# Attention inside a two-layer network: results of another head between a step's scores and sums, LN(x) tiles made in pairs and transposed a step later

## The chip, the cores and the metric

The kernel runs on one core of one Trainium2 chip. A core has a matrix engine (TensorE, in the profile PE, with its weight loads as PEld), three engines for everything else (VectorE, DVE; ScalarE, ACT; GpSimd, POOL) and SyncE (SP), which only issues DMAs. The engines run beside each other; each takes its own instructions in order and waits on semaphores for the others. The metric is the device time of one execution in microseconds (us); a lower time is better.

## The reference

Two layers on x of 4 x 32 x 32 tokens with 384 channels, all in float32. The part that the change touches is the first half of the first layer:

```python
qkv = _ln_c(x).reshape(B, N, C) @ qkv_w.T           # N = 1024 tokens, 12 heads of 32
attn = softmax(einsum('bhnd,bhmd->bhnm', q, k) * scale, axis=-1)
# 48 prototypes: every query chooses one; the mean query of each one marks 96 of the keys
final = row[..., :, None] * col[..., None, :]        # col: how many prototypes marked a key
attn = attn * final
attn = attn / (attn.sum(axis=2, keepdims=True) + 1e-08)   # over the queries
x = x + einsum('bhnm,bhmd->bhnd', attn, v)... @ proj_w.T
```

Then follow a mixture of four experts (two of them for a token), and a second layer with an outlook attention and a feed-forward part whose weights are Kronecker products. Attention is normalized twice: a softmax over the keys, then a division by the sum over the queries. So each score matrix is passed over twice, with two kinds of sums.

## The kernel before

`attention` walks through 4 images x 12 heads = 48 heads. A head is 4 steps (`PAIRS`), so there are 192 steps (`STEPS`), and the loop runs 9 more to finish. A step handles two blocks of 128 keys against all 1024 queries of a head. All instructions of TensorE, VectorE, ScalarE and SyncE are issued in the order in which the Python code writes them.

The parts of a step, with the names that the profile shows:

- **scores** (L597, tile `ps_s`): four matmuls, each on 32 rows of the array, into two PSUM tiles of 1024 columns. The pool `at_ps_s` has two such tiles, that is, one step's.
- **exps** (L607, tile `e`): two ScalarE instructions turn them into exponentials, in two tiles of the pool `at_e`.
- **total** (sums, L615 with tile `ps_z`): four matmuls, each on 32 columns of the array, add the exponentials up over the keys, in the one tile of `at_ps_z`.
- **gather** and **spread**: after a head's last sums, the sums go out to DRAM by two SyncE DMAs, come back in another layout, and their reciprocals are spread over all partitions (`rz`) by two more.
- **share** (L653 and L660): six steps later (`SHARE = 6`) VectorE multiplies the two tiles `e` in place with `rz` and with the column weights, sums them over the queries, and scales the values by the reciprocals, into `wv`.
- **out** (results, L615 with tile `ps_o`): seven steps later (`OUT = 7`) four matmuls with `wv` and the tiles `e` build the head's result in the one tile of `at_ps_o`. These are the last readers of the two tiles `e`.
- **keep** (L673, L680, L682): after a head's last results ScalarE copies `ps_o`, and four DMAs (two on SyncE, two adding ones on GpSimd) put the rows over those of the queries.

The pool of the exponentials has `EBUFS = 14` buffers. A tile's buffer is given to a new tile when all instructions that use the old one have been issued, and the new tile's first writer waits for the last of them on the chip.

Between the exponentials and the sums of a step, other work is put in. Some has fixed places: values (L690 to L695), projections of the image before (`project`), the loads and counts of the search for the 96 keys (`topk`: ScalarE's Sign at L351 once a step, its `load` at L306 and L310, `count` at L400). The rest comes from two generators, `groups` (prototypes: L517, L546, L561) and `prepare` (LN(x), then q and k). Each yields a cost in us and a condition before the next unit. In each step, units are taken while the account `spent` is below `goal`, and `goal` rises by `PACE = 2.6` a step but never to more than `MOST = 2.6` above `spent`, so a budget that is not used is lost:

```python
goal = min(goal + (RAMP if step < 12 else PACE), spent + MOST)
...
while spent < goal and prepared():
    pass
```

`prepare(b)` handles an image in two halves of four tiles of 128 tokens. For each half VectorE takes mean and variance, ScalarE the square root (L463), and then, tile by tile, ScalarE writes the normalized tile `xn` (L471, two buffers), TensorE transposes it (`turn`, L445, three blocks) into a PSUM tile, and ScalarE copies that into `xnT` (L446). After that come the q and k matmuls (L266), each followed by a copy (L501). The PSUM tiles of all this work come from `psum()`, which has two buffers. The transposes of a tile are issued behind the next tile's `xn`. `after(n)` is a condition that holds n steps after the unit became the next one.

Of the kernel before, what the change touches and what calls it, by code (L numbers as in the profile page):

```python
# [10 lines left out]
FP = mybir.dt.float32  # L11
AF = mybir.ActivationFunctionType
# [4 lines left out]
P = 128  # L17
B, IMG, C = 4, 32, 384
# [120 lines left out]
def attention(net, outer, router, x, x1, unsafe, qkv_wT, gpT, proj_wT, proj_w, gate_w, gate_b):  # L139
# [14 lines left out]
    tc, nc = net.tc, net.nc  # L154
    NHEAD = B * NH
    PAIRS = NB // 2
    STEPS = PAIRS * NHEAD
    SHARE, OUT = 6, 7
# [5 lines left out]
    with ExitStack() as ctx:  # L164
# [4 lines left out]
        work = ctx.enter_context(tc.tile_pool(name="at_work", bufs=2))  # L169
# [10 lines left out]
        def fetch(b, half, tag="xt"):  # L180
            xt = xts[b, half] = early.tile([P, 4, C], FP, name="xt", tag=tag)
            r = b * NTOK + 512 * half
            nc.sync.dma_start(out=xt, in_=x[r : r + 512, :].rearrange("(t p) c -> p t c", p=P))
# [58 lines left out]
        def gating():  # L242

            by = early.tile([P, KC, C], FP, name="proj", tag="xt")
            nc.scalar.dma_start(out=by, in_=proj_w.rearrange("(k p) i -> p k i", p=P))
            ps = psum()
            for k in range(KC):
                nc.tensor.matmul(
                    ps[:, :NE], lhsT=router.ones, rhs=gates[:, k, :], start=k == 0, stop=k == KC - 1
                )  # L250
            for c in range(KC):
                o = (c + 1) * NE
                for k in range(KC):
                    nc.tensor.matmul(
                        ps[:, o : o + NE], lhsT=by[:, k, c * P : (c + 1) * P], rhs=gates[:, k, :],
                        start=k == 0, stop=k == KC - 1,
                    )
            nc.scalar.copy(sums, ps[:, :NE])
            nc.scalar.copy(
                wproj[:, :, C:], ps[:, NE : (KC + 1) * NE].rearrange("p (c e) -> p c e", e=NE)  # L260
            )
# [18 lines left out]
        def after(steps):  # L280
            due = now[0] + steps
            return lambda: now[0] >= due

        spent = 0.0
        reached, heads, projected, valued = set(), [], set(), set()
# [141 lines left out]
        def prepare(b):  # L427

            im = images[b]
            yield 0, lambda: b == 0 or b - 1 in valued
            xnT = im["xnT"] = early.tile([P, KC, NTOK], FP, name="xnT", tag="xnT")
            for name in ("col", "inv"):
                im[name] = tiny.tile([P, NB, NH], FP, name=name, tag=name, bufs=2)
            nc.gpsimd.memset(im["col"], float(NG))
            im["mean"] = few.tile([P, NB], FP, name="mean", tag="mean", bufs=3)
            im["std"] = few.tile([P, NB], FP, name="std", tag="std", bufs=3)
            im["x"] = few.tile([P, NB, NE], FP, name="gate_x", tag="gate_x", bufs=3)  # L440

            def turn(xn, o):
                ps = psum()
                for c in range(KC):
                    nc.tensor.transpose(ps[:, c * P : (c + 1) * P], xn[:, c * P : (c + 1) * P], net.ident)  # L445
                nc.scalar.copy(xnT[:, :, o : o + P], ps[:, :C].rearrange("p (c t) -> p c t", c=KC))  # L446

            behind = None
            for half in range(2):
                if half and b:  # L450
                    yield 0, after(2)
                xt = xts.pop((b, half))
                mv = tiny.tile([P, 4, 2], FP, name="ln_mv", tag="ln_mv", bufs=2)
                rs = tiny.tile([P, 4], FP, name="ln_rs", tag="ln_rs", bufs=2)
                off = tiny.tile([P, 4], FP, name="ln_off", tag="ln_off", bufs=2)
                for t in range(4):
                    st = tiny.tile([P, 6], FP, name="ln_st", tag="ln_st", bufs=2)
                    nc.vector.bn_stats(st, xt[:, t, :])
                    nc.vector.bn_aggr(mv[:, t, :], st)
                    if t % 2:  # L460
                        yield 0.3, None
                std = im["std"][:, 4 * half : 4 * half + 4]
                nc.scalar.activation(std, mv[:, :, 1], AF.Sqrt, bias=net.eps["c"])  # L463
                yield 0.3, after(1) if b else None
                nc.vector.tensor_copy(im["mean"][:, 4 * half : 4 * half + 4], mv[:, :, 0])
                nc.vector.reciprocal(rs, std)
                nc.vector.scalar_tensor_tensor(off, mv[:, :, 0], -1.0, rs, ALU.mult, ALU.mult)
                for t in range(4):
                    yield 0.9, None
                    xn = work.tile([P, C], FP, name="xn", tag="xn")  # L470
                    nc.scalar.activation(  # L471
                        xn, xt[:, t, :], AF.Identity, bias=off[:, t : t + 1], scale=rs[:, t : t + 1]
                    )
                    if behind is not None:
                        turn(*behind)
                    behind = xn, (4 * half + t) * P
                if half == 0 and b:
                    fetch(b, 1)
                elif half and b + 1 < B:
                    if b == 0:  # L480
                        gating()
                    fetch(b + 1, 0)
            yield 0.9, None
            turn(*behind)
            for c in range(KC):
                yield 0, lambda: (
                    (b == 0 or len(heads) > NH * (b - 1) + 4 * c + 3)
                    and (b < 2 or len([p for p in projected if p[0] == b - 2]) == NB)
                )
                q = lasting.tile([P, NTOK], FP, name="q", tag="q", bufs=6)  # L490
                k = big.tile([P, NTOK], FP, name="k", tag="k", bufs=3)
                im["q"].append(q)
                im["k"].append(k)
                for out, base in ((q, 0), (k, C)):
                    for half in range(2):
                        yield 2.6, None
                        cols = slice(half * 512, half * 512 + 512)
                        ps = psum()
                        o = base + c * P
                        linear(ps, lambda k: wqkv[:, k, o : o + P], lambda k: xnT[:, k, cols])  # L500
                        nc.scalar.copy(out[:, cols], ps)  # L501
                reached.add((b, c, "qk"))
# [301 lines left out]
        step = -100  # L804
# [17 lines left out]
        goal = spent  # L822
        for step in range(STEPS + OUT + 2):
            n, u = divmod(step, PAIRS)
            if 0 <= step - OUT < STEPS:
                heads[(step - OUT) // PAIRS].out((step - OUT) % PAIRS)
                if (step - OUT) % PAIRS == PAIRS - 1:
                    heads[(step - OUT) // PAIRS].keep()
            if n < NHEAD:
                heads[n].scores(u)  # L830
            if u == 0 and 0 < n <= NHEAD:
                heads[n - 1].gather()
            if n < NHEAD:
                heads[n].exps()
            b, i = divmod(step, PAIRS * NH)
            goal = min(goal + (RAMP if step < 12 else PACE), spent + MOST)
            if u == 1 and 0 < n <= NHEAD:
                heads[n - 1].spread()
            begin(step)
            if step < 12:  # L840
                search()
                search()
            widen(step)
            o, t = i - OUT - 2, (i - OUT - 2) // 2
            if b and 0 <= o < 2 * NB and o % 2 == 0:
                project(b - 1, t)
            if b and 0 <= o + 1 < 2 * NB and o % 2:
                residue(b - 1, t + 1)
            if b and o > 2 * NB:
                next(routing[b - 1], None)  # L850
            if b < B:
                for t in {3: [0], 4: [1, 2], 5: [3], 6: [4], 7: [5, 6], 8: [7]}.get(i, []):
                    value(b, t)
            while spent < goal and prepared():
                pass
            if n < NHEAD:
                heads[n].total(u)
            if zeros and step >= 4:
                zeros.pop(0)()
            if 0 <= step - SHARE < STEPS:  # L860
                heads[(step - SHARE) // PAIRS].share((step - SHARE) % PAIRS)
            search()
            end()
            search()
            if u == 1 and n + 1 < NHEAD:
                heads.append(Head(n + 1))
# [1330 lines left out]
```

## Time and profile before

| what | value |
|---|---|
| median of 3 runs | 3002.94 us (3001.56 to 3003.22) |
| the profiled execution | 3008.57 us |
| its span, first to last instruction | 3006.7 us, granted TensorE clock 0.971 |
| TensorE (PE) busy | 2793.6 us, 93% |
| VectorE (DVE) busy | 1344.4 us, 45% |
| ScalarE (ACT) busy | 1222.3 us, 41% |
| GpSimd (POOL) busy | 396.4 us, 13% |
| first scores, last scores of the attention loop | 81.4 us, 1252.8 us |

Busy time is the union of an engine's instructions. In the timeline a line gives the start, the length, the engine, the line of the code, the operation with the tile that it writes and those that it reads, its tile of the array (for TensorE, rows x columns) and shape, and how many instructions are merged into it; in brackets stands the idle time before it and what ended it. One float32 matmul of the code shows as two records. In the table of waits a line gives who waited for what, the total, the number of times and the longest. In the table by stretch there are, for each engine, the busy time and the number of instructions, then the granted clock of TensorE, the share of the DMA engines and GB/s.

### The profile page before, as it was taken

The page shows a single profiled execution, that of the slowest core. Times are in us where ns is not written, and L with a number is a line of the kernel's source. Part 1 is how long each engine was busy: PE and PEld are TensorE (multiplying, and loading weights), DVE is VectorE, ACT ScalarE, POOL GpSimd, SP SyncE. Part 2 cuts the span into 40 slices and gives each one's busy share as a digit, 9 for nine tenths or more (in the row PEclk, how much of TensorE's full clock was granted, in tenths as well). Part 3 has the DMA queues.
Part 4 walks back from the last instruction along what each step waited for, and adds up shares of the span by engine and source line. Part 5 has one row for each costly group of instructions (what it writes and reads, how often), then busy time and mean ns, then how long its engine had stood idle before and what let it go on. Part 6 is the DMA issues. An engine that isn't in the chain of part 4 may idle for free.

```text
span 3006.7 us, 36661 instructions
## 1 busy us (share of the span) xinstructions
PE 2793.6 (93%) x13236; PEld 1509.9 (50%) x13236; DVE 1344.4 (45%) x3704; ACT 1222.3 (41%) x2026; POOL 396.4 (13%) x496
## 2 busy tenths in 40 slices
PE   6879998999899986689999999999999978999998
PEld 4323333333333331156777777777777744444443
DVE  1466677766776676633010001111111147767652
ACT  3777777776767765321112112111121122222125
POOL 1000000200030004014111112212211012000000
PEclk9989999999999998899999999999999989999999
DMA  5133334322322233254445545555555455544432
GB/s 100 52 81 98 92 92 122 78 54 68 93 56 54 77 90 118 49 200 155 169 177 189 186 174 204 213 211 196 201 215 210 142 170 190 163 165 139 157 112 86
DMA packets 218111, 405.91 MB, mean 135 GB/s; under 512 B 83504, under 2 KB 179296, under 8 KB 204864
## 3 DMA queue, kind: packets, MB, share of 16 engines
q1 hardware_dynamic: 188496, 194.43, 21.7%
q0 software_dynamic: 26432, 206.01, 20.1%
q10 hardware_dynamic: 2992, 3.03, 0.3%
q8 instruction: 107, 1.75, 0.2%
q14 instruction: 84, 0.69, 0.1%
HBM read 305.35 MB, written 49.99 MB: 118 GB/s over the span
## 4 chain that ended last, share of the span: by engine, by line
PE 78%; ACT 7%; DVE 6%; DMA 5%; issue 4%; POOL 0%; SPq 0%; DVEq 0%; POOLq 0%; ACTq 0%
PE ps_h L1568 18%; PE ps_y L1583 17%; PE ps_t L266 7%; PE ps_z L615 7%; PE ps_s L597 6%; PE ps_o L615 5%; PE ps_a L1693 4%; ACT e L607 4%; PE ps_y L1795 3%; DVE e L653 2%; PE ps_wo L1811 2%; DMA yt<-yg,index 2%; PE ps_v L1737 1%; PE ps_h L1964 1%; PE ps_t L400 1%
## 5 line engine op out<-in xcount | busy, mean ns | idle before, releaser
L1572 ACT ACTIVATE h<-ps_h,up 128x256 f32<-128x256 f32 x420 | 199.0, 474 | 929.2 <-PE ps_h L1568 929.2
L1568 PE MATMUL ps_h<-xbT,up 128*128 128x256 f32 x2520 | 556.8, 382 | 0.8 <-DVE xbT L1527 0.7
L1583 PE MATMUL ps_y<-down,h 128*128 128x384 f32 x1680 | 556.8, 489 | 0.0
L1568 PEld LDWEIGHTS ps_h<-xbT,up 128*128 128x128 f32 x2520 | 482.4, 192 | 76.9 <-DVE xbT L1527 1.1
L653 DVE CUSTOM_DVE_ANT_0 e<-e,rz,inv 128x1024 f32<-128x1024 f32 x384 | 474.3, 1272 | 65.1 <-DMA rz<-r_row 64.8
L607 ACT ACTIVATE e<-ps_s,shift 128x1024 f32<-128x1024 f32 x384 | 406.7, 1110 | 192.2 <-PE ps_s L597 191.9
L1583 PEld LDWEIGHTS ps_y<-down,h 128*128 128x128 f32 x1680 | 318.5, 191 | 208.2 <-issue 3.3
L1588 DVE TENSOR_TENSOR y<-ps_y,down 128x384 f32<-128x384 f32 x70 | 39.0, 558 | 755.6 <-PE ps_y L1583 755.6
L615 PE MATMUL ps_z<-e,rt_ones 128*32 128x512 f32 x1536 | 295.1, 631 | 62.8 <-ACT e L607 62.8
L615 PE MATMUL ps_o<-e,wv 128*32 128x512 f32 x1536 | 273.9, 634 | 27.2 <-DVE wv L660 15.6
L597 PE MATMUL ps_s<-q,k 32*128 32x512 f32 x1536 | 222.9, 650 | 0.0
L680 POOL DMA_DIRECT2D q<-po x96 | 75.7, 874 | 1058.2 <-DMA q<-po 622.2
L351 ACT ACTIVATE below<-tk_left,tk_bound 128x1024 bf16<-128x1024 f32 (+1 forms) x160 | 183.8, 1149 | 12.1 <-DVE tk_bound L357 7.6
L1693 PE MATMUL ps_a<-wa,xnT 128*128 128x486 f32 x384 | 172.2, 595 | 10.7 <-DVE attn L1703 10.0
L615 PEld LDWEIGHTS ps_z<-e,rt_ones 128*32 128x32 f32 x1536 | 45.6, 109 | 228.4 <-ACT e L607 190.0
L597 PEld LDWEIGHTS ps_s<-q,k 32*128 32x128 f32 x1536 | 61.5, 187 | 169.5 <-issue 135.1
L615 PEld LDWEIGHTS ps_o<-e,wv 128*32 128x32 f32 x1536 | 66.4, 114 | 150.5 <-issue 108.7
L266 PE MATMUL ps_t<-xnT,wqkv 128*128 128x512 f32 x288 | 138.1, 621 | 2.8 <-ACT tk_left L310 1.8
L1693 PEld LDWEIGHTS ps_a<-wa,xnT 128*128 128x128 f32 x384 | 72.4, 195 | 96.7 <-issue 89.6
L1795 PE MATMUL ps_y<-band,v 128*32 128x194 f32 (+2 forms) x960 | 108.4, 516 | 4.1 <-DMA band<-room 3.9
L1538 DVE SCALAR_TENSOR_TENSOR x<-yt,weight,x 128x384 f32<-128x384 f32 x38 | 23.5, 619 | 191.9 <-DMA x<-x 191.3
L1507 POOL DMA_INDIRECT xb<-x,ids x70 | 66.9, 955 | 251.4 <-PE ps_t L1526 218.4
(331 smaller groups left out, 2860.6 us busy)
## 6 DMA issues: line engine op xcount, KB each, us to landing
band<-room SPq DMA_DIRECT2D x32, 1560.0 KB
rz<-r_row SPq DMA_DIRECT2D x48, 512.0 KB
yg<-y SPq DMA_DIRECT2D x70, 192.0 KB
q<-q SPq DMA_DIRECT2D x192, 64.0 KB
k<-k SPq DMA_DIRECT2D x192, 64.0 KB
room<-none SPq DMA_DIRECT2D x64, 192.0 KB
x<-x SPq DMA_DIRECT2D x38, 192.0 KB
o<-in_x_dram SPq DMA_DIRECT2D x33, 192.0 KB
```

Source lines behind the costliest of these rows:

```text
L266: nc.tensor.matmul(ps, lhsT=lhsT(k), rhs=rhs(k), start=k == 0, stop=k == KC - 1)
L351: nc.scalar.activation(junk[:n], left[:n], AF.Sign, bias=bound[:n], accum_out=over[:n])
L597: nc.tensor.matmul(ps[:, half * 512 : half * 512 + 512], lhsT=self.k4[r, u * P : (u + 1) * P], rhs=self.q4[r, :], start=True, stop=True,)
L607: nc.scalar.activation(e, ps, AF.Exp, bias=shift, scale=QK_SCALE)
L615: nc.tensor.matmul(ps[r : r + 32, :], lhsT=lhsT(odd), rhs=self.es[2 * u + odd][:, half * 512 : half * 512 + 512], start=u == 0, stop=u == ...
L653: nc.vector.tensor_tensor_reduce(self.es[m], self.es[m], self.rz, 1.0, self.im["inv"][:, m, self.h : self.h + 1], ALU.mult, ALU.add, self. ...
L680: nc.gpsimd.dma_start(out=there, in_=po[r : r + 32, :], accum_op=ALU.add)
L1568: nc.tensor.matmul(ps, lhsT=up[:, o : o + P], rhs=xbT[:, k, :], start=k == 0, stop=k == KC - 1,)
L1572: nc.scalar.activation(h, ps, AF.Gelu, bias=up[:, KC * HID + f : KC * HID + f + 1])
L1583: nc.tensor.matmul(ps, lhsT=hs[f][:, t * P : (t + 1) * P], rhs=down[:, f * C : (f + 1) * C], start=f == 0, stop=f == NF - 1,)
L1693: nc.tensor.matmul(pa[:, hh, :HW_], lhsT=xnT[:, k, :], rhs=wa[:, k, hh * HW_ : (hh + 1) * HW_], start=k == 0, stop=k == KC - 1,)
L1795: nc.tensor.matmul(ys[c][32 * n : 32 * n + 32, lo - 512 * half : hi - 512 * half], lhsT=vs[b, t][:, h * HD : (h + 1) * HD], rhs=bands[b, t ...
```

## The change

In the step loop, the results of seven steps before (`out`, and `keep` when a head ends) are issued after the scores, the gather and the exponentials of the step, where they were issued before the scores. In `prepare`, a unit makes two tiles `xn` where it made one, and it begins with the transposes of the two tiles that the unit before made. From the second image on, such a unit comes at the earliest one step after the unit before. The costs follow: five units of 1.8 in an image, where there were nine of 0.9.

```diff
-            behind = None
+            behind = []
...
-                for t in range(4):
-                    yield 0.9, None
-                    xn = work.tile([P, C], FP, name="xn", tag="xn")
-                    nc.scalar.activation(
-                        xn, xt[:, t, :], AF.Identity, bias=off[:, t : t + 1], scale=rs[:, t : t + 1]
-                    )
-                    if behind is not None:
-                        turn(*behind)
-                    behind = xn, (4 * half + t) * P
+                for two in range(2):
+
+                    yield 1.8, after(1) if b else None
+                    while behind:
+                        turn(*behind.pop(0))
+                    for t in (2 * two, 2 * two + 1):
+                        xn = work.tile([P, C], FP, name="xn", tag="xn")
+                        nc.scalar.activation(
+                            xn, xt[:, t, :], AF.Identity, bias=off[:, t : t + 1], scale=rs[:, t : t + 1]
+                        )
+                        behind.append((xn, (4 * half + t) * P))
...
-            yield 0.9, None
-            turn(*behind)
+            yield 1.8, after(1) if b else None
+            while behind:
+                turn(*behind.pop(0))
...
             n, u = divmod(step, PAIRS)
-            if 0 <= step - OUT < STEPS:
-                heads[(step - OUT) // PAIRS].out((step - OUT) % PAIRS)
-                if (step - OUT) % PAIRS == PAIRS - 1:
-                    heads[(step - OUT) // PAIRS].keep()
             if n < NHEAD:
                 heads[n].scores(u)
             if u == 0 and 0 < n <= NHEAD:
                 heads[n - 1].gather()
             if n < NHEAD:
                 heads[n].exps()
+            if 0 <= step - OUT < STEPS:
+                heads[(step - OUT) // PAIRS].out((step - OUT) % PAIRS)
+                if (step - OUT) % PAIRS == PAIRS - 1:
+                    heads[(step - OUT) // PAIRS].keep()
```

## The prediction

> **What bounds the kernel now.** I read the page's totals first, then TensorE's waits in the attention stage, then the timeline of single steps.
>
> ```profile
> PE 2793.6 (93%) x13236; PEld 1509.9 (50%) x13236; DVE 1344.4 (45%) x3704; ACT 1222.3 (41%) x2026; POOL 396.4 (13%) x496
> ```
>
> TensorE is the busy engine, but this is an average over stages. The change touches only the attention loop, whose 192 steps run from 81 to 1257 us. There, from 123 us on (the first results) to 1255 us, the waits of TensorE are:
>
> ```profile
> PE ps_z L615 <- ACT e L607: 57.9, 63, 3.0
> PE ps_t L445 <- ACT xn L471: 25.4, 10, 4.3
> ...
> PE ps_o L615 <- DVE topped L390: 5.6, 1, 5.6
> ```
>
> The columns are total us, times and longest. Sums wait for exponentials, and the transposes of LN(x) wait for their tile: the two things that the change moves. How a step runs is seen in two kinds of steps. The first has plenty of other matmuls:
>
> ```profile
> 657.59 1.06 PE L615 MATMUL ps_z<-e,rt_ones 128*32 128x512 f32 x8
> 658.48 1.04 PE L615 MATMUL ps_o<-e,wv 128*32 128x512 f32 x8
> 659.45 1.14 PE L597 MATMUL ps_s<-q,k 32*128 32x512 f32 x8
> 660.52 0.70 PE L266 MATMUL ps_t<-xnT,wqkv 128*128 128x512 f32 x1
> ```
>
> From start to start, sums take 0.89, results 0.97, scores 1.07, then other work follows without a gap. Ninety-eight of the 184 steps 7 to 190 are longer than the floor shown next. The second kind has little other work:
>
> ```profile
> 302.71 1.14 PE L597 MATMUL ps_s<-q,k 32*128 32x512 f32 x8
> 303.78 0.92 PE L546 MATMUL ps_t<-gpbd,q 128*128 128x192 f32 x4
> 305.05 1.63 PE L615 MATMUL ps_z<-e,rt_ones 128*32 128x512 f32 x6 [0.35 <-ACT e L607]
> 306.07 0.62 PE L615 MATMUL ps_o<-e,wv 128*32 128x512 f32 x2
> ...
> 307.90 0.71 PE L597 MATMUL ps_s<-q,k 32*128 32x512 f32 x4
> ```
> ```profile
> 303.89 2.12 ACT L607 ACTIVATE e<-ps_s,shift 128x1024 f32<-128x1024 f32 x2 [1.95 <-PE ps_s L597]
> ```
>
> Scores at 302.71, exponentials from 303.89 to 306.01, the second half of the sums and the results behind it, the next scores at 307.90: 5.19 us. Eighty-six steps have this length to 0.05 us whatever else they hold; it is the ring scores, exponentials, sums, results, scores.
>
> **The new order in a step.** Its aim is to let results (four calls, eight records) fill the wait for the exponentials. One number stands against that. A step makes two e tiles, results run OUT = 7 steps behind their scores, and EBUFS = 14. In the old order the results of step s-7 have been issued when step s takes its two tiles. In the new order `exps` asks for them while `out(s-7)`, the last reader of the two oldest, is still ahead: all 14 are live. So ScalarE's exponentials wait for the results, and behind them in ScalarE's queue everything else of the step: the copy of ps_o, which now follows them, copies out of PSUM, the search's Sign. TensorE's sums wait for all of it. The ring keeps its members in another order: scores, results, exponentials, sums. Its length from the rows: scores to results 1.07; results end 1.04 after they start and the exponentials follow a matmul's end by 0.04 (302.71 + 1.14 to 303.89), so they start at 2.15 and end at 4.27; the second half of the sums starts 0.06 later (306.01 to 306.07) and holds TensorE for two of its passes and a change to the scores' shape, 0.44 + 0.53 = 0.97: 5.30 us, 0.11 more than 5.19.
>
> In the 98 longer steps the change of the array's tile shape counts. In a step of the old order that has other work the shape changes three times (128*128 to 128*32, to 32*128, and back; sums and results share one shape), in the new order four times. The first steps, which have no results yet, show sums between two changes:
>
> ```profile
> 112.74 1.07 PE L615 MATMUL ps_z<-e,rt_ones 128*32 128x512 f32 x8
> 113.74 1.14 PE L597 MATMUL ps_s<-q,k 32*128 32x512 f32 x8
> ```
>
> That is 1.00 instead of 0.89. Results between two changes are not in this trace; by the same row they take 1.00 instead of 0.97. Sums and results then take 2.00 instead of 1.86: 0.14 a step. Results into 128*128 could cost as little as 0.97 or as much as the scores' 1.07, so the bounds are 0.10 and 0.24; 1.00 is the same operation, so I take it. Sum: 86 x 0.11 + 98 x 0.14 = 9.5 + 13.7 = 23 us.
>
> Something comes back where results were late for another reason. TensorE waited 15.0 us in 11 waits for VectorE before results; the scores now run meanwhile, at most 1.07 each, 7.7 us together; half of it, 4, since VectorE's lateness also reaches the next step. Where ScalarE itself is late (before 29 of the 192 pairs of exponentials it was not idle for scores), results hide; most lie in the LN steps below, so I take 2. The new order costs 23 - 6 = 17 us, bounds 10 and 28.
>
> The keeping of a head's results (step u = 2) now stands behind the exponentials: a copy of 0.59, two SyncE and two GpSimd DMAs start some 2.7 us later. ScalarE's idle time before exponentials (191.9 us in all) hides the copy; without it 48 x 0.59 = 28 us. The nearest reader of these rows, `project`, comes 21 us after the copy (412.22 to 433.36). No other SyncE issue of that step waits on it for long: gather and Head issue at u = 0 and 1. Cost 0.
>
> **LN(x) tiles in pairs.** Before, one step takes up to three units, each a tile and the transposes of the tile just before, which stands behind the step's exponentials in ScalarE's queue:
>
> ```profile
> 473.63 0.55 PE L445 MATMUL ps_t<-ident,xn 128*128 128x128 f32 x3
> 476.53 1.88 PE L445 MATMUL ps_t<-ident,xn 128*128 128x128 f32 x6 [2.35 <-ACT xn L471]
> 478.34 1.83 PE L615 MATMUL ps_z<-e,rt_ones 128*32 128x512 f32 x8
> ```
> ```profile
> 473.11:476.52 3.41, 1.07 (x11) 0.31 (x3) 1.78 (x7) 2.76 (x4) 0.00 (x0) 1.00 0.14 21
> 476.52:479.93 3.41, 3.33 (x14) 1.40 (x18) 2.97 (x8) 3.40 (x7) 0.00 (x0) 0.50 0.22 53
> ```
>
> The second fence is the table by stretch; the last three columns are granted clock, DMA share and GB/s. After a wait of 2.35 us the clock halves for 3.41 us and the sums take 1.66 to the next start instead of 0.89. Ten steps of images 1 to 3 hold such waits or late tiles; by the starts of their scores they take 10.0, 7.1, 10.3, 10.6, 8.4, 7.7, 9.0, 10.4, 7.8 and 8.8 us, 90 together, where floor or own matmuls give 53. So 37 us are at stake, 25.4 of them plain waits less what the ring hides, the rest slow clock. The Trainium skill, "TensorE: Matmul & The Clock Gate", section "Why this matters for your kernels", asks only for no idle gaps above about 3 us between bursts; by that the 2.35 us waits would cost no clock, and the gain below would be an estimated 8 us less. The rows show the clock falling after 2.35 us, and they decide.
>
> After, an image has five units, at least a step apart (`after(1)`), so a transpose never waits for a tile of its own step. A pair step gives ScalarE 2.12 of exponentials, two copies of 0.48, two tiles of 0.70 and a Sign of 1.34, overlapping by a tenth each: about 5.4, next to the ring. I worked through the loop's budget (PACE 2.6, units of 1.8, the conditions on each): transposes fall in steps 14, 18, 19, 20, 65, 71, 72, 73, 114, 120, 121, 122. What is late there next is PSUM: psum() has two buffers, emptied behind the exponentials. In 20 and 114 a search's load fills both, and transposes wait for copies (exponentials end 4.27, copy 0.59, against matmuls done at 3.94): 1.7 us with the second one. In 73 and 122 a q unit follows two transposes and waits for the 0.48 copy, 4.85 against 2.73: 2.1. Step 14 has a score whose buffer VectorE empties last: 1.5; 65 and 71 with a projection 0.5; the five others 0.2. That is 11; two slow clock stretches 3; q and k units two to four steps later, partly into full steps, 3. The first image has no exponentials in the way: 0. Gain 37 - 17 = 20 us; bounds 8, if the waits for tiles turn into waits for copies and the clock stays low, and 32.
>
> **The sum.** +17 - 20 = -3 us on a span of 3006.7 in an execution of 3008.57 (1.9 us outside). That execution is 5.6 us above the median of 3002.94, so I apply the difference to the median: 3000 us. A difference under 0.2% (6 us) cannot be told from none.
>
> **Rivals.** *PSUM takes the place of the tile* (slower): the gain is at its bound of 8, the order costs 17 to 28: +14, 3017 us. It decides once the gain falls under 11. For it: the copies stand behind the same exponentials; against it: five of the twelve steps need no third buffer, and in three more it costs only 0.5 to 1.5. *Results hide more* (faster): order +10, gain 28: 2985 us. *The change does what it says*, exponentials do not wait for results: the ring loses 0.97 of results to the overlap, 86 x 0.86 = 74, less VectorE's own chain of row DMAs: some 50 us, 2950 us. Against it stands 14 = 2 x 7.
>
> **How the numbers follow.** Forecast, within 6 us of before: 0.40. PSUM rival 0.28, and 0.02 for a dearer shape change: slower 0.30. Results hide more 0.25, no wait for e tiles 0.05: faster 0.30. The range runs from both good bounds (+10 - 32 = -22, 2981) to both bad ones (+28 - 8 = +20, 3023).
>
> **What would show it.** Ring steps of 5.30 with exponentials starting some 2.15 after scores, released by results; sums and results at 1.00 each; no wait of L445 for xn in images 1 to 3, but waits for copies L446 or L310; fewer half-clock stretches between 158 and 820 us. Ring steps near 4.4 would refute the wait for e tiles; an order cost above 28 or L445 waits of 20 us would refute the sum.

## The result, and the profile after

The changed kernel takes 3023.5 us (median of 8 runs, 3016.5 to 3026.6) against 3004.0 us for the kernel before beside it: a ratio of 1.0053, 95% interval 1.004 to 1.0065. Ratios here are of the mean times; microseconds that are given for a ratio are its part of 3004 us. It is slower by half a per cent, 16 us by the ratio, where 3000 us and no clear change were forecast. The profiled execution took 3026.56 us, its span 3024.8 us, at a granted clock of 0.973. The lines of the `prepare` hunk push the later code down by three: scores are L600 now, exponentials L610, sums and results L618.

The page's totals and its group of the exponentials (the last part of that line is the idle time before them and what ended it):

```profile
PE 2814.4 (93%) x13236; PEld 1482.2 (49%) x13236; DVE 1345.2 (44%) x3704; ACT 1218.5 (40%) x2026; POOL 393.9 (13%) x496
...
L610 ACT ACTIVATE e<-ps_s,shift 128x1024 f32<-128x1024 f32 x384 | 406.7, 1110 | 257.6 <-PE ps_o L618 256.1
```

TensorE is busy for 20.8 us more with the same 13236 matmul records. Before, the scores ended ScalarE's idle time ahead of the exponentials (191.9 of 192.2 us); now the results end 256.1 of 257.6 us.

TensorE's waits between 80 and 1290 us:

```profile
PE ps_z L618 <- ACT e L610: 75.4, 71, 4.6
...
PE ps_o L618 <- DVE tk_parts L355: 8.3, 2, 4.2
...
PE ps_t L266 <- ACT xnT L446: 5.6, 2, 3.9
...
PE ps_t L445 <- DVE g L533: 3.0, 1, 3.0
PE ps_t L445 <- ACT tk_left L310: 2.3, 2, 1.3
...
PE ps_t L445 <- DVE gate_o L724: 1.5, 2, 1.0
```

The 25.4 us in which transposes waited for `xn` are gone. The waits that came in their place are 12.4 us (5.6, 3.0, 2.3 and 1.5), all of it for PSUM tiles that ScalarE or VectorE had not emptied yet. The wait of the sums for the exponentials, which the new order was to fill, grew to 75.4 us, from 62.8 in the same window before.

A ring step in the timeline, the answer to the step at 302.71 before:

```profile
296.21 1.14 PE L600 MATMUL ps_s<-q,k 32*128 32x512 f32 x8
...
297.28 1.06 PE L618 MATMUL ps_o<-e,wv 128*32 128x512 f32 x8
...
298.38 2.12 ACT L610 ACTIVATE e<-ps_s,shift 128x1024 f32<-128x1024 f32 x2 [1.12 <-PE ps_o L618]
...
301.54 0.71 PE L600 MATMUL ps_s<-q,k 32*128 32x512 f32 x4
```

The exponentials start 2.17 us after the scores, released by the results. From scores to scores it takes 5.33; 85 steps have this length to 0.05. A longer step, TensorE alone:

```profile
578.01 1.14 PE L600 MATMUL ps_s<-q,k 32*128 32x512 f32 x8
579.08 1.07 PE L618 MATMUL ps_o<-e,wv 128*32 128x512 f32 x8
580.08 0.92 PE L549 MATMUL ps_t<-gpbd,q 128*128 128x192 f32 x4
...
583.50 1.06 PE L618 MATMUL ps_z<-e,rt_ones 128*32 128x512 f32 x8
584.50 1.14 PE L600 MATMUL ps_s<-q,k 32*128 32x512 f32 x8
```

Results take 1.00 to the next start and sums 1.00. This step is 6.49 long, where one with the same work took 6.35.

**Where the 16.6 us of the loop went.** From the first scores to the last the loop takes 1187.9 us instead of 1171.3. The starts of the scores give the length of every step; the table adds them up by stretches. The last column takes 0.13 us a step off (from step 7 on), which is what the undisturbed steps lost to the order, 0.11 to 0.14 each.

| steps | what falls there | before | after | difference | less 0.13 a step |
|---|---|---|---|---|---|
| 11 to 23 | LN(x) of image 1 | 89.2 | 81.7 | -7.5 | -9.2 |
| 24 to 47 | its q, k, prototypes | 136.3 | 145.3 | +9.0 | +5.9 |
| 62 to 77 | LN(x) of image 2 | 103.1 | 103.6 | +0.6 | -1.5 |
| 78 to 95 | its q, k, prototypes | 106.6 | 110.9 | +4.2 | +1.9 |
| 109 to 123 | LN(x) of image 3 | 99.5 | 94.5 | -5.0 | -7.0 |
| 124 to 145 | its q, k, prototypes | 132.2 | 145.0 | +12.8 | +10.0 |
| the others | | 504.5 | 506.9 | +2.4 | -7.4 |

The order's share is 184 steps by 0.13, 24 us. The other steps come to 7.4 less than that; TensorE's waits for VectorE before results fell by 3.9 (27.3 to 23.4 in the window above), and the rest of the 7.4 was not taken apart. The three stretches of LN(x) gain 17.7 us, and the three behind them lose 17.8.

Two things limit what these two sums say. Two executions of one kernel differ: the run base below, which is the kernel before once more, has 4.2 us less in the LN stretches and 1.4 more in those behind; against it the three sums are -13.4, +16.4 and -9.1. And part of the work only crossed the line: steps 19, 120, 121 and 123 held a q or k unit before and hold none after, and 5.7 us of the gain are theirs. The total of both kinds of stretches, 0 (+3 against base), is free of this: the pairs were to bring 20 us and brought none.

### The profile page after: what moved, and what is told of

Read it like the earlier page. It is cut to its first block, busy times and chain, and to the rows that moved or that the text cites. A ratio compares the mean times of both kernels' runs of the same rounds, so it can differ in the third digit from the quotient of the medians.

```text
span 3024.8 us, 36673 instructions
## 1 busy us (share of the span) xinstructions
PE 2814.4 (93%) x13236; PEld 1482.2 (49%) x13236; DVE 1345.2 (44%) x3704; ACT 1218.5 (40%) x2026; POOL 393.9 (13%) x496
## 4 chain that ended last, share of the span: by engine, by line
PE 78%; ACT 7%; DVE 6%; DMA 5%; issue 3%; POOL 0%; SPq 0%; DVEq 0%; ACTq 0%; POOLq 0%
PE ps_h L1571 17%; PE ps_y L1586 17%; PE ps_t L266 8%; PE ps_z L618 7%; PE ps_s L600 5%; PE ps_o L618 5%; PE ps_a L1696 4%; ACT e L610 3%; PE ps_y L1798 3%; DVE e L656 2%; PE ps_wo L1814 2%; DMA yt<-yg,index 2%; PE ps_v L1740 1%; PE ps_t L400 1%; PE ps_h L1967 1%
## 5 line engine op out<-in xcount | busy, mean ns | idle before, releaser
L610 ACT ACTIVATE e<-ps_s,shift 128x1024 f32<-128x1024 f32 x384 | 406.7, 1110 | 257.6 <-PE ps_o L618 256.1
L618 PE MATMUL ps_z<-e,rt_ones 128*32 128x512 f32 x1536 | 296.5, 626 | 75.4 <-ACT e L610 75.4
L618 PE MATMUL ps_o<-e,wv 128*32 128x512 f32 x1536 | 213.6, 627 | 26.4 <-DVE wv L663 12.5
L600 PE MATMUL ps_s<-q,k 32*128 32x512 f32 x1536 | 225.0, 656 | 0.0
L351 ACT ACTIVATE below<-tk_left,tk_bound 128x1024 bf16<-128x1024 f32 (+1 forms) x160 | 184.2, 1151 | 17.7 <-DVE col L416 12.6
L618 PEld LDWEIGHTS ps_z<-e,rt_ones 128*32 128x32 f32 x1536 | 45.8, 109 | 249.8 <-ACT e L610 203.8
L600 PEld LDWEIGHTS ps_s<-q,k 32*128 32x128 f32 x1536 | 61.8, 188 | 168.5 <-issue 168.5
L618 PEld LDWEIGHTS ps_o<-e,wv 128*32 128x32 f32 x1536 | 31.1, 110 | 180.1 <-issue 83.5
L1455 POOL DMA_INDIRECT yt<-yg,index x64 | 67.0, 1047 | 246.3 <-DVE x L1541 143.1
```

The lines of the kernel that those rows point to most:

```text
L351: nc.scalar.activation(junk[:n], left[:n], AF.Sign, bias=bound[:n], accum_out=over[:n])
L600: nc.tensor.matmul(ps[:, half * 512 : half * 512 + 512], lhsT=self.k4[r, u * P : (u + 1) * P], rhs=self.q4[r, :], start=True, stop=True,)
L610: nc.scalar.activation(e, ps, AF.Exp, bias=shift, scale=QK_SCALE)
L618: nc.tensor.matmul(ps[r : r + 32, :], lhsT=lhsT(odd), rhs=self.es[2 * u + odd][:, half * 512 : half * 512 + 512], start=u == 0, stop=u == ...
```

## The experiments

The theory after the result had two parts. The order costs because 14 buffers make the exponentials wait for the results, and because the array's tile shape changes once more. The pairs gain what was forecast and give it back, because q and k units and the prototypes that follow from them come later and meet other work. The rival: all the late losses are the order's, which makes ScalarE and VectorE late. The kernels came in three groups (order, pairs and the two trims; base, near, e15 and near15; late, zrz and ord15). Each group shared a chip and the runs of the kernel before; ratios are against those.

### The two halves apart

*order*: the loop as changed, `prepare` as before. *pairs*: `prepare` as changed, the loop as before.

```diff
 order:
-            if 0 <= step - OUT < STEPS: ... out, keep      (ahead of scores)
+            if 0 <= step - OUT < STEPS: ... out, keep      (behind exps)
 pairs:
-                for t in range(4): yield 0.9, None ...
+                for two in range(2): yield 1.8, after(1) if b else None ...
```

> The new order alone, with LN(x) as before. Theory: the order costs about 0.13 us in each of some 184 steps (ring steps 5.32, longer steps 0.14 dearer), 23 us, and the LN steps and what comes after them stay as they were: 3003 + 20 to 24 = 3023 to 3027 us. Rival: the losses that the changed kernel shows behind its LN steps (some 18 us in steps 24 to 48, 78 to 96 and 124 to 146) are the order's too, since all that stands behind the exponentials on ScalarE and VectorE comes later: +35 to +41, 3038 to 3044 us.

> The pairs of LN(x) tiles alone, with the results ahead of the scores as before. Theory: the LN steps gain some 17 us (no transpose waits for its tile), and the steps behind them lose about as much, because the q and k units come two to four steps later and fall into full steps: 3003 with 5 us either way. Rival (the losses are the order's): the 17 to 20 us stay, 2983 to 2986 us.

Measured: order 3049.4 us, ratio 1.0071 (1.0057 to 1.0084); pairs 3031.8 us, ratio 1.0007 (0.9995 to 1.0019); the kernel before took 3027.5 us on this chip. The order costs 0.71%, 21 us on 3004; the pairs change nothing measurable. Both fall to the theory and neither to the rival. In the trace of order 84 steps are 5.33 long and its exponentials wait for the results; in that of pairs 74 steps keep 5.19.

By stretches, as in the table above, order loses 18.0 us behind LN(x), which looks like the rival's. But 16.6 of it stand in steps 81, 82 and 130, where the engines pause on this chip (last section). Of the 1.4 that are left, 5.9 are lost in steps 24 to 47 and 4.5 gained in the other two stretches. The pairs gain 20.1 in the LN stretches and lose 36.4 behind them, 17.9 of it in the pauses of steps 81, 82 and 129; 18.5 are left. So the loss behind comes in the main with the pairs and not with the order. Single steps differ: step 46 loses 2 us in order and in the changed kernel, and nothing in pairs.

### The buffers of the exponentials

*trim16* is the changed kernel with 16 buffers, and *trim14* the same with 14. Both need room, which single buffers make.

```diff
-EBUFS = 14
+EBUFS = 16                                  # trim14 leaves it at 14
-po = work.tile([P, 512], ..., tag="po", bufs=1)
+po = work.tile([P, 512], ..., tag="zr", bufs=1)
-self.rz = work.tile([P, NTOK], ..., tag="rz")
+self.rz = work.tile([P, NTOK], ..., tag="rz", bufs=1)
 (also: one buffer for "o", "logit", "logit_part"; two for "wv")
```

> The changed kernel with 16 buffers for the exponentials, so that a step's exponentials need not wait for its results; the room comes from single buffers for rz, the residual rows and the logits, one buffer for zr and po, two for wv. Theory (the wait for e tiles is what keeps the results from hiding the wait for the exponentials): exponentials start 1.2 us after the scores instead of 2.15, released by the scores; ring steps fall from 5.32 to 4.3 to 4.6, where VectorE and the row DMAs allow it; 2950 to 2985 us. Rival (the step's length is set by ScalarE's or VectorE's own work, and the wait only shows where the slack was): ring steps stay over 5.1, and the time is within 5 us of the same kernel with 14.

> The same single buffers with 14 buffers for the exponentials: a control for the run with 16. Theory: these buffers had slack, and the time is that of the changed kernel, 3020 to 3027 us. Rival: one buffer for rz makes its row DMA wait for the shares of the head before, VectorE comes late once a head, 48 x 0.5 to 1 us: 3045 to 3070 us.

Measured: trim16 3008.5 us, ratio 0.9932 (0.9917 to 0.9947); trim14 3056.0 us, ratio 1.0095 (1.008 to 1.0111). Two more buffers are worth 47 us. On 3004 us, trim16 stands at 2984, at the upper end of what its theory said. The exponentials are released by the scores again (114.6 of 140.1 us of idle time), and 29 steps take 4.33. So the wait for `e` tiles was what kept the results from filling the gap. The control shows that the single buffers were not free: some 12 us on top of the changed kernel (3032 us on 3004, between the theory's 3027 and the rival's 3045). One of them shows in SyncE's waits of trim14, and not in those of the changed kernel:

```profile
SPq L650 <- DVE d L661: 46.9, 40, 3.8
```

The DMA that fills the one `rz` waits for the head before to finish with it. How much of the 12 us this wait makes, and how the rest divides among the single buffers, was not tried.

### Fifteen buffers are enough

*e15* is the changed kernel with 15 buffers, which fit without touching `rz`: the first exponential of a step finds a free buffer, and by the time the second starts the results are done.

```diff
-EBUFS = 14
+EBUFS = 15
 (po in the buffer of zr; one buffer for "o", "logit", "logit_part"; two for "wv")
```

> The changed kernel with 15 buffers for the exponentials instead of 14; the room comes from one buffer for the residual rows and the logits, one for zr and po together, two for wv; rz keeps both. The first exponential of a step then has a free buffer, and the second needs the results only when the first ends. Theory: as good as 16 in the ring (second exponential 1.11 after the first, results end 2.15 after the scores), without the single rz: 30 to 40 us under the kernel before. Rival (two free buffers are needed): no better than the changed kernel, some 16 us over the kernel before.

Measured: 2979.3 us, ratio 0.9919 (0.9900 to 0.9937): 24 us under the kernel before, less than the theory said, far from the rival's 16 over. Of its ring steps 32 take 4.33. Much of what is missing went into one step of 20.9 us, in which the copy `zr` waits 17.4 us. The run near15 (below) has such a step too, of 24.5; its lines for ScalarE and TensorE in the timeline:

```profile
1169.57 0.59 ACT L632 COPY zr<-ps_z 128x512 f32<-128x512 f32 x1 [21.00 <-DMA q<-po]
...
1171.22 2.93 PE L618 MATMUL ps_z<-e,rt_ones 128*32 128x512 f32 x8 [19.49 <-ACT e L610]
```

`zr` shares a buffer with `po`, whose adding DMAs stand on GpSimd behind those of the router. In near15 a buffer saved this way cost TensorE a wait of 19.5 us once.

### Does the delay of q and k eat the gain?

*base* is the kernel before, unchanged, for a trace beside the others. *near* is pairs with two amendments that keep q and k units near their old steps. *late* is the kernel before with nothing but their delay.

```diff
 near:
-                    yield 1.8, after(1) if b else None
+                    yield 1.8, after(1) if b and two else None
...
-            yield 1.8, after(1) if b else None
+            yield 2.6, after(1) if b else None
 late:
-                    (b == 0 or len(heads) > ...)
+                    (c > 0 or now[0] >= (-100, 22, 74, 122)[b])
+                    and (b == 0 or len(heads) > ...)
```

> The kernel before, unchanged, traced on the chip of this group of runs: the chip of the first group took 3027.5 us for it instead of 3003, and its traces show steps of 10 to 17 us beside the 17 indirect DMAs that each image's router issues on GpSimd. Theory: these stalls belong to the chip; the kernel before shows them too there (three places, 20 to 27 us together), while its ring steps stay 5.19 us. Rival: the stalls come with the edits, and the kernel before has none.

> The pairs of LN(x) alone (results ahead of the scores), with two amendments: the first pair of a half may stand in the step of its offsets, and the last transposes cost 2.6, so that no q unit shares their step. By the account q and k units then fall at most one step later than in the kernel before, where the pairs alone put them two to four later. Theory (the pairs' gain of some 17 us is given back by q and k units in full steps): 13 to 18 us under the kernel before. Rival (it is given back by something else, for example by the copies that the transposes wait for): no change within 5 us.

> The kernel before with nothing but a delay: the first q unit of an image waits until step 22, 74 or 122 (images 1 to 3), where the changed kernel has its first ones; it stands at 18, 72 and 120 before. LN(x) and the order of the results stay as they were. Theory (the pairs' gain goes because the q and k units, and with them the prototypes, fall into steps that are full already): 12 to 18 us over the kernel before. Rival (the delay is free, since the budget of a step is the same wherever a unit falls): within 4 us of it.

Measured: base 3002.4 us (one run; 3001.4 the median of its group); near 2995.9 us, ratio 0.9975 (0.9963 to 0.9987); late 3015.6 us, ratio 1.0029 (1.0012 to 1.0046). Both go the theory's way, and both by about half of what it said: near is 7.5 us faster (4 to 11 by the interval) where 13 to 18 were expected and the rival allowed 5, late 8.7 slower (4 to 14) where 12 to 18 were and the rival allowed 4. So a delay alone costs time, but less than the theory said. The stretches, summed from the traces of near and late against that of base (which ran on the chip of near):

| | LN stretches | stretches behind | others |
|---|---|---|---|
| near - base | -20.7 | +12.7 | -2.0 |
| late - base | -4.1 | +14.6 | -6.2 |
| after - before, less 0.13 a step | -17.7 | +17.8 | -7.4 |

The delay alone, without a line of LN(x) or of the order changed, costs 14.6 us in the stretches behind, and gets 4.1 back because the LN steps lose units (step 18 falls from 10.37 to 6.27): 10.5 together. Not all of this is a unit in a step that was full. In step 79 of late, 5.1 us longer than in base, a prototype's matmuls join the search's counts, but TensorE also runs at half the clock (0.50 from 572.60 to 582.92 us) after a wait for VectorE at the end of the step before, which was 0.37 us in base:

```profile
571.60 1.07 PE L616 MATMUL ps_o<-e,wv 128*32 128x512 f32 x8 [2.72 <-DVE tk_parts L355]
...
572.60 2.09 PE L598 MATMUL ps_s<-q,k 32*128 32x512 f32 x8
```

Whether that wait follows from the delay is not shown. With the amendments the loss behind is 12.7, not zero. Here the expectation was wrong about its own kernel: the q and k units were to come at most one step later, but in the trace the first two of image 1 stand in steps 20 and 22, where base has them in 18 and 19. Step 20 holds a search's `load` as well and takes 8.72 instead of 5.21. So the amendments recover part; what it would take to recover the rest is not shown.

The base run was to show whether the stalls of the first group's chip (last section) are the chip's. It ran on another chip, had none, and leaves that open.

### Both halves mended

*near15* joins e15 and near. *zrz* gives `po` its own buffer back and puts `zr` into the half of `rz` that is filled only later. *ord15* is zrz with LN(x) as before.

```diff
 zrz, in gather:
-zr = work.tile([P, 512], ..., tag="zr", bufs=1)
+self.rz = work.tile([P, NTOK], ..., tag="rz")
+zr = self.rz[:, :512]
 zrz, in spread:
-self.rz = work.tile([P, NTOK], ..., tag="rz")
```

> The changed order with 15 buffers and the pairs of LN(x) with both amendments of the run near. Theory: the two gains add, since one shortens ring steps and the other LN steps: e15 less 10 to 15 us, 40 to 55 us under the kernel before. Rival: with the ring shorter, VectorE and the row DMAs of the reciprocals set the step, and the second gain is lost: within 5 us of e15.

> The run near15 with zr in the first half of the buffer that rz takes a little later, instead of in one buffer with po. In near15 the copy zr waited 21 us for the GpSimd DMAs of po, which stood behind the router's 17 indirect DMAs; TensorE lost 19.5 us in that one step. Theory: that wait goes, and the time falls 15 to 25 us below near15, 45 to 55 us under the kernel before. Rival (the step then waits for something else that the router holds): within 5 us of near15.

> The new order with 15 buffers for the exponentials as in zrz, but LN(x) as in the kernel before: the order alone, once its exponentials need not wait. Theory: the amended pairs are worth 8 to 15 us on top of it, so it stands 35 to 42 us under the kernel before. Rival (with results that hide a wait, the transposes' waits for their tile hide as well, and the pairs are worth nothing): within 4 us of zrz.

| run | us | ratio | interval |
|---|---|---|---|
| near15 | 2971.2 | 0.9899 | 0.9884 to 0.9914 |
| ord15 | 2962.3 | 0.9857 | 0.9842 to 0.9872 |
| zrz | 2946.3 | 0.9812 | 0.9793 to 0.9830 |

near15 missed its 40 to 55 us (30), because the expectation did not know of the shared buffer; without it, zrz is 57 us under the kernel before, 26 better than near15 by the ratios, a little more than was expected of it (45 to 55, and 15 to 25). The order with its buffer is worth 43 us alone (ord15), and the amended pairs 14 on top: they are not hidden by the results. The ring of zrz, from the page and the timeline:

```profile
L610 ACT ACTIVATE e<-ps_s,shift 128x1024 f32<-128x1024 f32 x384 | 406.6, 1109 | 105.1 <-PE ps_s L600 94.8
```
```profile
1131.21 1.14 PE L600 MATMUL ps_s<-q,k 32*128 32x512 f32 x8
...
1132.28 1.06 PE L618 MATMUL ps_o<-e,wv 128*32 128x512 f32 x8
1132.39 2.12 ACT L610 ACTIVATE e<-ps_s,shift 128x1024 f32<-128x1024 f32 x2 [0.76 <-PE ps_s L600]
...
1135.54 0.71 PE L600 MATMUL ps_s<-q,k 32*128 32x512 f32 x4
```

The exponentials start 1.18 after the scores, the results run beside them, and the step takes 4.33. Thirty-nine steps do; the loop is 1118.4 us instead of 1171.3.

## Why the prediction was wrong, step by step

- **The order, +17 (bounds 10 to 28): right.** Ring steps were forecast at 5.30 with exponentials 2.15 after the scores; they are 5.33 and 2.17. The shape change was forecast at 1.00 each for sums and results and 0.14 a step; that is what the rows show. By the table it is 24 less a remainder of 7.4, where 23 less 6 were forecast. The order alone measured +21 us (17 to 25).
- **No wait for e tiles, rival at 0.05: rightly held unlikely** for this kernel. Its estimate of some 50 us under the kernel before, for a kernel without that wait, is near what ord15 had (43).
- **The steps of the transposes: right.** In the trace they stand in the twelve steps that the prediction named.
- **The waits that replace the tile, 11: right in sum as waits.** TensorE waited 12.4 us, at the steps named: 14 (a score's buffer, 3.0 instead of 1.5), 20 and 114 (the search's load, 2.3 instead of 3.4), 65 and 71 (1.5 instead of 1.0), 73 and 122 (the copy of `xnT`, 5.6 instead of 4.2).
- **The two steps with a q unit behind two transposes, 2.1 each: too small for step 122.** The wait was 1.8 us in step 73 and 3.9 in step 122, which took 12.15 us. ScalarE and TensorE in it:

```profile
834.48 2.12 ACT L610 ACTIVATE e<-ps_s,shift 128x1024 f32<-128x1024 f32 x2
...
836.49 0.59 ACT L676 COPY po<-ps_o 128x512 f32<-128x512 f32 x1
837.10 1.28 ACT L746 ACT_TABLE_LOAD   x1
838.39 0.30 ACT L746 ACTIVATE o_rs<-mv,eps_t 128x8 f32<-128x8 f32 x1
838.60 0.84 ACT L446 COPY xnT<-ps_t 128x384 f32<-128x384 f32 x2
...
839.11 4.42 PE L266 MATMUL ps_t<-xnT,wqkv 128*128 128x512 f32 x6 [3.86 <-ACT xnT L446]
```

The copy of `po`, which the new order put behind the exponentials and which was costed at nothing, a table load of 1.28 and the router's square root stand ahead of the copy that frees PSUM. TensorE waits 3.86, the clock is 0.59 in the mean from 838.3 to 841.7 us, and the q matmuls take 4.42 instead of the 2.84 of step 122 before. The copy of `po` is the smaller part: in the run pairs, where it comes earlier, the step takes 11.77. The table load and the square root, 1.5 us together, are the larger; they stood behind the exponentials of step 122 before, too, and the prediction left them out of this queue.

- **"q and k units two to four steps later, partly into full steps, 3": this step failed.** The units do come later, by up to four steps. The stretches behind LN(x) lose 17.8 us in the changed kernel; without the 5.7 of the units that only left an LN step, some 12 are left (11 against base), and 2 of these are the order's, in step 46. The run late, in which nothing but the delay was changed, lost 8.7 (4 to 14), and 10.5 by its trace. So the term is about 10, not 3. The prediction had followed the account as far as the step in which each transposing unit falls and did not go on to the prototypes, scores and means that follow from q and k. In the traces a q or k unit costs 0.5 us in a step that holds little else (late, step 24: 5.70 instead of 5.21) and 3.5 beside a search's `load` (near, step 20).
- **"11 for waits and 3 for slow clock": too small by as much.** The ten slow steps fell from 90.0 to 56.7 us, 33 of the 37 that were at stake. But the other LN steps, apart from the four that lost a unit, took 23 us more after 0.13 a step, where 14 were forecast. Steps 14, 73 and 122 alone took 14.4 more; the clock was 0.83 in step 73 and 0.86 in step 122. The waits alone were near the forecast, so most of the error is in what else these steps took; how it divides was not tried.
- **The clock.** The forecast took it from one place that a wait of 2.35 us halves the clock. The trace of before shows both: in step 64 such a wait is followed by a clock of 0.50 (the rows of the prediction), in step 72 the clock stays at 1.00 in the mean of the step:

```profile
529.35 0.55 PE L445 MATMUL ps_t<-ident,xn 128*128 128x128 f32 x3 [2.35 <-ACT xn L471]
```

Nor can the sign that was named be put down to the change. Between 158 and 820 us the trace of before has 44 us below full clock and that of after 27, but the run base, the same kernel as before, has 27 as well. How much of the gain was clock stays open.

- **The sum and the rivals.** Forecast: 17 - 37 + 14 + 3 = -3. By the same terms the traces give 16.5 for the order, -34.7 for the ten steps, +22.7 for the other LN steps and +12.1 for the later units: +16.6. Against base the ten steps are -31, so a few us of each term are the scatter of one execution. The medians differ by 19.5. The time came out on the side of the slower rival (3017 us) and past it. That rival's mechanism, the copies that free PSUM, explains part of the miss at most: these waits came to 12.4 us where the forecast had 11, and all that the LN steps took beyond the forecast is 9 us, as much as the later units.

## What to carry to other kernels

When two instructions of a step change places, count the live buffers at the new place of the allocation: a ring that exactly covers the distance (14 = 2 x 7) turns an overlap into a wait, and one more buffer can be worth more than the whole edit. When work is made cheaper but later, follow everything that depends on it through the rest of the schedule, step by step; here 33 us were gained in the ten steps that were looked at, and all of it was paid back in others. Before two tiles share a buffer to make room, see which queue frees each: here one stood behind the router's DMAs, and the other tile waited 21 us.

## What the runs showed of the hardware

- **A change of the array's tile shape** shows in the rows: four sums take 0.89 us to the next start beside results of the same shape and 1.00 between two changes; results 0.97 and 1.00. The Trainium skill ("TensorEngine Tiling (Array Packing)", section "Key Properties") says that changing the mode drains TensorE. One more change a step cost 0.14 us in these rows (sums and results 1.86 before, 2.00 after).
- **Stalls of all engines beside the router's indirect DMAs, on one chip.** The chip of the first group took 3027.5 us for the kernel before. The traces of its four kernels have steps of 10 to 18 us while GpSimd issues the 17 DMAs into the router's table. In the run order:

```profile
600.48 1.11 ACT L607 ACTIVATE e<-ps_s,shift 128x1024 f32<-128x1024 f32 x1 [5.74 <-PE ps_t L266]
...
601.65 1.05 PE L615 MATMUL ps_z<-e,rt_ones 128*32 128x512 f32 x4 [2.18 <-issue]
...
604.02 1.11 ACT L607 ACTIVATE e<-ps_s,shift 128x1024 f32<-128x1024 f32 x1 [2.42 <-remote]
...
607.54 0.56 DVE L528 TENSOR_REDUCE g_max<-ps_t 128x8 f32<-128x384 f32 x1 [11.36 <-remote]
```

TensorE, ScalarE and VectorE pause together, with releases that the profile cannot place. The step takes 13.12 us, where the same step takes 6.35 before and 6.49 after on other chips. The traces on two other chips have no such pauses beside these DMAs. The kernel before has no trace on this chip, so whether the chip or the edits bring the pauses stays open, and what holds the engines was not found.
